# Packing a spectrum of 192 channels into 128 partitions with column tiles

## The chip, the cores and the metric

The kernel runs on one core of one Trainium2 chip, as one program. The metric is the device time in microseconds (us), the median of three runs. A run with the hardware profiler gives the profile and the trace from which all views below are taken. TensorE is called PE in them, its weight loads PEld, VectorE DVE, ScalarE ACT, GpSimd POOL and the queue that issues the transfers SP.

## The reference

Thirty-two images of 56x56 positions with 96 channels pass through two layers. The first is a layer norm, a 3x3 convolution and a SiLU with a residual. The second treats the 3136 positions of an image as a sequence, and has a spectral attention and a quantized feed-forward network. The part that the change touches is in the spectral attention:

```
h = relu(bn1(x @ w1.T))                      # 96 -> 192 channels
X = fft(h, axis=positions)                   # a transform per channel
xr = relu(X.real * rd - X.imag * idg + rb)   # rd, idg, rb, ib: one number per channel
xi = relu(X.imag * rd + X.real * idg + ib)
y = ifft(xr + 1j * xi).real
o = y @ w2.T                                 # 192 -> 96 channels, then bn2
```

All of this is float32. Since y is real, the transform back keeps one half of a Hermitian spectrum; the kernel folds that into two terms for the real and imaginary part of each stored frequency.

## The kernel before

**The transform in two factors.** 3136 is split into 112 x 28. `transform_a` multiplies by w1 and does the first factor (112 points) and writes the result to a buffer `da` in memory; read back transposed, it is ready for the second factor (28 points). The 56 first-factor frequencies are handled in 28 pairs, `PG = 4` pairs are one unit, and an image has `NS = 7` units, so the kernel has 32 x 7 = 224 units.

**One unit of `spectrum`.** `back` brings the unit's rows, `ats[g]`, with 112 partitions by 4 pairs by 192 channels. `forward(g, i)` runs for i = 0 and i = 1, the two halves of 96 channels: four matmuls (line 379), one per pair, each with 96 channels as the stationary operand and a table of 112 columns (`fb_sb`, 114 in the first unit of an image) as the moving one. The result `px` has the 96 channels on the partitions and 4 pairs x 2 (real, imaginary) x 56 frequencies along the free dimension. Then come three ACT instructions (lines 389 to 391, into `av`), three DVE instructions (lines 393 to 395, into `sv`), one more ACT instruction (line 396) and two DVE instructions (lines 397 and 398) that write `gt`, all on 96 partitions by 224 elements, with the channel's numbers as per-partition scalars out of `par_sb` and `scal`.

`inverse(g)` runs a step later. For each of the four pairs it multiplies `gt` (96 channels by 112 frequencies, the stationary operand) with w2 (96 columns, the moving operand), for i = 0 and i = 1 into the same accumulator `pg`: eight matmuls (line 406). ACT copies the accumulator to `gw` (line 408), four matmuls with `ib_sb` do the second factor back (line 411, `pe`), ACT copies that to `es` (line 413), and a transfer brings it to the buffer `de`.

**Records of one matmul.** A float32 matmul of this program stands in the trace as two weight loads and two MATMUL records; 224 units x 8 matmuls of `px` are 3584 records. A transpose has one record. A record is called a pass below.

**What else runs.** A loop over the images is a pipeline by hand: while an image's spectrum runs, `filler` emits parts of the convolution of a later image (`conv_part`: lines 328 to 337) and of its input (`take_in`, `make_image`: lines 257 to 299). After the spectrum stage the loop emits, group by group, `forth` (the next image's `transform_a`), `back` (the transform out, line 431) and `ffn` (lines 437 to 460). A scheduler then orders the instructions of each engine by its own estimates, so the order on an engine is not the order of the source. `px` shares the accumulators of tag "c" (two buffers) with `ph` and `py`; `pg` and `pe` share tag "b" (two buffers) with `pa` and `po`.

Of the kernel before, what the change touches and what calls it, by code (L numbers as in the profile page):

```python
# [38 lines left out]
F32 = mybir.dt.float32  # L39
# [3 lines left out]
ALU = mybir.AluOpType  # L43
AX = mybir.AxisListType

C = 96
# [5 lines left out]
PG = 4  # L52
NS = NP // PG
H = 192
# [8 lines left out]
LN_CHUNKS = ((0, 8), (8, 16), (16, 24), (24, 28))  # L63


LN_W, LN_B, CONV_B, B_IN, BN1, BN2, RD, RB, NPAR = 0, 1, 2, 3, 5, 13, 17, 21, 25


def width(p):

    return 2 * N2 + (p < PG)


def first(p):

    return 2 * (2 * N2 * p + min(p, PG))


@with_exitstack
def hybrid_kernel(ctx: ExitStack, tc: tile.TileContext, x, par, w_in, conv_w, w1, w2, fw1, fb1, fw2, fb2, fa, fb, ib, ia, on, out):  # L80
    nc = tc.nc
    nb = x.shape[0]

    const = ctx.enter_context(tc.tile_pool(name="const", bufs=1))


    ident = const.tile([128, 128], F32, name="ident")
# [8 lines left out]
    fb_sb = const.tile([112, first(NP)], F32, name="fb_sb")  # L96
    ib_sb = const.tile([114, NP, 112], F32, name="ib_sb")

    par_sb = const.tile([C, NPAR], F32, name="par_sb")
    nc.sync.dma_start(par_sb, par)  # L100
    convb = par_sb[:, CONV_B : CONV_B + 1]

    wp = const.tile([128, 7, C], F32, name="wp")
    w1a = const.tile([C + 1, H], F32, name="w1a")
    w2a = const.tile([C, 2, C], F32, name="w2a")
    w1q = const.tile([C, FF], F8, name="w1q")
    w2q = const.tile([128, 3, C], F8, name="w2q")
    b1q = const.tile([128, 3], F32, name="b1q")
# [2 lines left out]

    stages = [const.tile([C, 2, G4, P58], F32, name=f"stage{i}") for i in range(2)]
    ys = [const.tile([113, G4, C], F32, name=f"y{i}") for i in range(4)]
    scal = const.tile([C, 3, 2], F32, name="scal")

    dconst = ctx.enter_context(tc.tile_pool(name="dconst", bufs=1, space=bass.MemoryType.DRAM))
    imgs = [dconst.tile([C, (P58 + 1) * P58], F32, name=f"img{i}") for i in range(3)]
# [1 line left out]
    with tc.tile_pool(name="setup", bufs=1) as sp, tc.tile_pool(  # L119
        name="setup_ps", bufs=2, space=bass.MemoryType.PSUM  # L120
# [13 lines left out]
        for g in range(2):  # L134
            ps = spp.tile([128, 512], F32, tag="ps", name=f"ps_wt{g}")
# [6 lines left out]
        for k in range(9):  # L142
            ps = spp.tile([128, 512], F32, tag="ps", name=f"ps_we{k}")
# [12 lines left out]
        def bn_fold(scale, bias, at, n):  # L156

            p = par_sb[:, at : at + 4 * n]
            nc.vector.tensor_scalar(scale, p[:, 3 * n : 4 * n], EPS, None, ALU.add)
            nc.gpsimd.tensor_tensor(scale, scale, mhalf[:C, :n], ALU.pow)  # L160
            nc.vector.tensor_tensor(scale, scale, p[:, 0:n], ALU.mult)
            nc.vector.tensor_tensor(bias, p[:, 2 * n : 3 * n], scale, ALU.mult)
            nc.vector.tensor_tensor(bias, p[:, n : 2 * n], bias, ALU.subtract)
# [7 lines left out]
        for g in range(2):  # L171
            nc.vector.tensor_scalar(w1s[:, g, :C], w1s[:, g, :C], s1[:, g : g + 1], None, ALU.mult)
            nc.vector.tensor_copy(w1s[:, g, C : C + 1], o1[:, g : g + 1])
            ps = spp.tile([128, 512], F32, tag="ps", name=f"ps_w1{g}")
            nc.tensor.transpose(ps[: C + 1, :C], w1s[:, g, :], ident[:C, :C])
            nc.vector.tensor_copy(w1a[:, g * C : (g + 1) * C], ps[: C + 1, :C])
        ps = spp.tile([128, 512], F32, tag="ps", name="ps_w1c")
# [4 lines left out]
        s2 = sp.tile([C, 1], F32, name="s2")  # L182
        o2 = sp.tile([C, 1], F32, name="o2")
        bn_fold(s2, o2, BN2, 1)
        w2s = sp.tile([C, H], F32, name="w2s")
        nc.sync.dma_start(w2s, w2)
        nc.vector.tensor_scalar(w2s, w2s, s2, None, ALU.mult)
        for g in range(2):
            ps = spp.tile([128, 512], F32, tag="ps", name=f"ps_w2{g}")
            nc.tensor.transpose(ps[:C, :C], w2s[:, g * C : (g + 1) * C], ident[:C, :C])  # L190
            nc.vector.tensor_copy(w2a[:, g, :], ps[:C, :C])
        ps = spp.tile([128, 512], F32, tag="ps", name="ps_o2")
        nc.tensor.transpose(ps[:1, :C], o2, ident[:C, :C])
        row = sp.tile([1, G4, C], F32, name="row")
# [3 lines left out]
            nc.sync.dma_start(y[112:113], row)  # L198


        nc.vector.tensor_scalar(scal[:, 0, :], par_sb[:, RD : RD + 2], 2.0, None, ALU.mult)
        nc.vector.tensor_scalar(scal[:, 1, :], par_sb[:, RB : RB + 2], 2.0, None, ALU.mult)
        nc.vector.tensor_scalar(scal[:, 2, :], par_sb[:, RD : RD + 2], -1.0, None, ALU.mult)


        f1 = sp.tile([128, 3, C], F32, name="f1")
# [3 lines left out]
        for k in range(3):  # L210
            ps = spp.tile([128, 512], F32, tag="ps", name=f"ps_f1{k}")
            nc.tensor.transpose(ps[:C, :128], f1[:, k, :], ident)
            nc.vector.tensor_copy(w1q[:, k * 128 : (k + 1) * 128], ps[:C, :128], saturate=False)
            ps = spp.tile([128, 512], F32, tag="ps", name=f"ps_f2{k}")
# [28 lines left out]
    work = ctx.enter_context(tc.tile_pool(name="work", bufs=2))  # L243
    w3 = ctx.enter_context(tc.tile_pool(name="w3", bufs=3))
    sums = ctx.enter_context(tc.tile_pool(name="sums", bufs=8))
    psum = ctx.enter_context(tc.tile_pool(name="psum", bufs=1, space=bass.MemoryType.PSUM))
    psum2 = ctx.enter_context(tc.tile_pool(name="psum2", bufs=2, space=bass.MemoryType.PSUM))
# [112 lines left out]
    def spectrum(da, de, b):  # L360


        rows = da.rearrange("n (k p) c -> (n k) p c", p=NP)
        gt, ats = {}, {}

        def back(g):
            ats[g] = w3.tile([112, PG, H], F32, tag="at", name=f"at_{b}_{g}")
            nc.sync.dma_start(ats[g], rows[:, g * PG : (g + 1) * PG, :])

        for g in range(3):  # L370
            back(g)
        yield

        def forward(g, i):
            w = width(g * PG)
            px = psum2.tile([C, PG, 2, w], F32, tag="c", name=f"px_{b}_{g}_{i}")
            for j in range(PG):
                p = g * PG + j
                nc.tensor.matmul(  # L379
                    px[:, j], ats[g][:, j, i * C : (i + 1) * C], fb_sb[:, first(p) : first(p + 1)], start=True, stop=True  # L380
                )
            if i == 0:
                gt[g] = w3.tile([C, 2, PG, 2, w], F32, tag="gt", name=f"gt_{b}_{g}")
            rd, idg = par_sb[:, RD + i : RD + i + 1], par_sb[:, RD + 2 + i : RD + 3 + i]
            rb, ibi = par_sb[:, RB + i : RB + i + 1], par_sb[:, RB + 2 + i : RB + 3 + i]
            rd2, rb2, mrd = (scal[:, k, i : i + 1] for k in range(3))
            re, im = px[:, :, 0, :], px[:, :, 1, :]
            av = work.tile([C, 3, PG, w], F32, tag="av", name=f"av_{b}_{g}_{i}")
            nc.scalar.activation(av[:, 0], im, AF.Abs, scale=idg)
            nc.scalar.activation(av[:, 1], re, AF.Relu, scale=rd2, bias=rb2)  # L390
            nc.scalar.activation(av[:, 2], re, AF.Identity, scale=idg, bias=ibi)  # L391
            sv = work.tile([C, 3, PG, w], F32, tag="sv", name=f"sv_{b}_{g}_{i}")
            nc.vector.scalar_tensor_tensor(sv[:, 0], re, rd, av[:, 0], ALU.mult, ALU.add)  # L393
            nc.vector.scalar_tensor_tensor(sv[:, 1], im, mrd, av[:, 2], ALU.mult, ALU.add)
            nc.vector.scalar_tensor_tensor(sv[:, 2], im, rd, av[:, 2], ALU.mult, ALU.add)  # L395
            nc.scalar.activation(sv[:, 1], sv[:, 1], AF.Relu)
            nc.vector.scalar_tensor_tensor(gt[g][:, i, :, 0, :], sv[:, 0], rb, av[:, 1], ALU.add, ALU.max)
            nc.vector.scalar_tensor_tensor(gt[g][:, i, :, 1, :], sv[:, 2], 0.0, sv[:, 1], ALU.max, ALU.subtract)  # L398

        def inverse(g):  # L400
            k = 2 * width(g * PG)
            pg = psum2.tile([k, PG, C], F32, tag="b", name=f"pg_{b}_{g}")
            for j in range(PG):
                for i in range(2):
                    lhs = gt[g][:, i, j].rearrange("c r k -> c (r k)")
                    nc.tensor.matmul(pg[:, j, :], lhs, w2a[:, i, :], start=(i == 0), stop=(i == 1))  # L406
            gw = work.tile([k, PG, C], F32, tag="gw", name=f"gw_{b}_{g}")
            nc.scalar.copy(gw, pg)
            pe = psum2.tile([112, PG, C], F32, tag="b", name=f"pe_{b}_{g}")
            for j in range(PG):  # L410
                nc.tensor.matmul(pe[:, j, :], ib_sb[:k, g * PG + j, :], gw[:, j, :], start=True, stop=True)  # L411
            es = work.tile([112, PG, C], F32, tag="es", name=f"es_{b}_{g}")
            nc.scalar.copy(es, pe)
            nc.sync.dma_start(de[g * PG : (g + 1) * PG].rearrange("p m c -> m p c"), es)
            del gt[g]

        for g in range(NS + 1):
            if g < NS:
                forward(g, 0)
                forward(g, 1)  # L420
            if g + 3 < NS:
                back(g + 3)
            yield
            if g >= 1:
                inverse(g - 1)
            yield
# [297 lines left out]
```

## Time and profile before

| what | value |
|---|---|
| device time, median of 3 | 4036.05 us (4034.21 to 4038.8) |
| span of the profiled execution | 4024.5 us, granted TensorE clock 0.982 |
| PE busy | 3664.8 us, 91% |
| PE weight loads busy | 2484.2 us, 62% |
| DVE busy | 2667.9 us, 66% |
| ACT busy | 2193.7 us, 55% |
| POOL busy | 1285.9 us, 32% |
| mean rate of the transfers | 137 GB/s |

A share of busy time is a mean over stages with different limits. The first `px` record starts at 203.0 us and the last at 3957.8 us, and between them the stages of the images repeat about every 120 us. The end of a PE record is modelled and records overlap, so a row's count times its mean is more than its busy time; the distance from one start to the next is what a pass takes of the engine.

### The profile page before, as it was taken

Reading aid. Unit: us, or ns where it says so; the run is one execution under the profiler, and the core shown is the slowest. Engines: PE = TensorE matmul, PEld = TensorE weight load, DVE = VectorE, ACT = ScalarE, POOL = GpSimd, SP = SyncE. Lnnn points to the kernel's source line nnn. Section 1 sums busy time; section 2 is a strip of 40 time slices with the busy share of each in tenths; the row PEclk is TensorE's granted clock in tenths of the full one; section 3 lists DMA queues with packets and bytes.
Section 4 is the critical chain, followed back from the end, with each engine's and each line's share of the span. In section 5 each row is a group of like instructions: output and inputs, shape, how many; then the busy total and the mean of one; then the engine's idle time right before and its main releaser. Section 6 shows DMA issues by size and latency. Waiting matters only on the chain. (4 is left out here: it accounts for less than half of the span.)

```text
span 4024.5 us, 70610 instructions
## 1 busy us (share of the span) xinstructions
PE 3664.8 (91%) x22229; PEld 2484.2 (62%) x22229; DVE 2667.9 (66%) x9014; ACT 2193.7 (55%) x5154; POOL 1285.9 (32%) x1004
## 2 busy tenths in 40 slices
PE   3899999999999999999999999999999999999987
PEld 2466665666665666665666655666655666665665
DVE  2256776766776766776766776766776766776666
ACT  0355555565555555555555555655555555555564
POOL 1222333332333332333322333322333332333222
PEclk9999999999999999999999999999999999999996
DMA  5454455555555555555545455545455555455531
GB/s 152 128 143 135 129 148 143 146 139 137 136 140 143 149 138 137 136 139 141 145 136 138 129 145 144 148 136 138 130 149 144 147 139 136 134 142 144 143 88 52
DMA packets 582156, 550.04 MB, mean 137 GB/s; under 512 B 171960, under 2 KB 534680, under 8 KB 581272
## 3 DMA queue, kind: packets, MB, share of 16 engines
q1 hardware_dynamic: 579906, 543.45, 49.5%
q8 instruction: 180, 2.95, 0.3%
q10 hardware_dynamic: 1880, 2.09, 0.2%
q14 instruction: 190, 1.56, 0.1%
HBM read 346.93 MB, written 197.99 MB: 135 GB/s over the span
## 5 line engine op out<-in xcount | busy, mean ns | idle before, releaser
L328 PE MATMUL cv<-k,wp 128*96 128x448 f32 (+1 forms) x3136 | 1370.5, 551 | 19.3 <-ACT s L330 12.6
L328 PEld LDWEIGHTS cv<-k,wp 128*96 128x96 f32 (+1 forms) x3136 | 463.2, 165 | 382.6 <-issue 326.3
L443 ACT CAST h<-pf 128x448 f16<-128x448 f32 x672 | 358.5, 533 | 434.3 <-PE pf L441 413.9
L432 DVE TENSOR_TENSOR t<-py,t 112x384 f32<-112x384 f32 x224 | 124.2, 555 | 628.3 <-PE py L431 628.3
L280 POOL TENSOR_TENSOR xn_c<-t,mu_c 112x768 f32<-112x768 f32 (+1 forms) x128 | 169.1, 1321 | 1027.2 <-DVE var_a L263 826.3
L379 PE MATMUL px<-fb_sb,at 112*96 112x112 f32 (+1 forms) x3584 | 429.6, 262 | 24.9 <-DVE sv L395 19.1
L379 PEld LDWEIGHTS px<-fb_sb,at 112*96 112x96 f32 x3584 | 382.4, 164 | 78.6 <-issue 31.6
L406 PE MATMUL pg<-w2a,gt 96*112 96x96 f32 (+1 forms) x3584 | 416.0, 264 | 13.0 <-DVE gt L398 10.8
L354 ACT ACTIVATE h<-ph,rs_b 112x192 f32<-112x192 f32 x896 | 325.0, 419 | 187.0 <-PE ph L351 175.9
L453 PEld LDWEIGHTS <-hq 128*112 128x112 fp8e5 x2688 | 209.0, 135 | 330.8 <-DVE hq L446 281.2
L351 PE MATMUL ph<-w1a,n2t 97*112 97x192 f32 x1792 | 366.0, 333 | 42.3 <-DVE t L432 41.6
L406 PEld LDWEIGHTS pg<-w2a,gt 96*112 96x112 f32 (+1 forms) x3584 | 382.3, 179 | 27.4 <-PE st L336 12.9
L269 POOL TENSOR_TENSOR rs_a<-var_a,mhalf 112x8 f32<-112x8 f32 (+1 forms) x128 | 199.4, 1558 | 610.9 <-DVE var_a L268 566.2
L445 DVE TENSOR_SCALAR h<-h,b1q 128x448 f16<-128x448 f16 x672 | 350.9, 522 | 62.7 <-ACT h L443 59.3
L330 ACT ACTIVATE s<-cv,par_sb 96x448 f32<-96x448 f32 x224 | 141.4, 631 | 457.3 <-PE cv L328 457.3
L453 PE MATMUL po<-w2q,hq 128*112 128x96 fp8e5 x2688 | 252.2, 221 | 141.3 <-DVE hq L446 133.2
L269 POOL TENSOR_TENSOR rs_b<-var_b,mhalf 112x8 f32<-112x8 f32 (+1 forms) x128 | 192.5, 1504 | 580.7 <-DVE var_b L268 414.5
L356 PE MATMUL pa<-h,fa_sb 112*112 112x384 f32 x896 | 369.4, 508 | 6.3 <-ACT h L354 1.2
L460 POOL TENSOR_TENSOR o<-t,y 112x384 f32<-112x384 f32 x224 | 201.1, 898 | 449.5 <-DVE y L459 259.7
L351 PEld LDWEIGHTS ph<-w1a,n2t 97*112 97x112 f32 x1792 | 281.7, 177 | 93.7 <-DVE t L432 61.1
L446 DVE CAST hq<-h 128x448 fp8e5<-128x448 f16 x672 | 314.8, 469 | 16.1
L393 DVE SCALAR_TENSOR_TENSOR sv<-px,par_sb,av 96x224 f32<-96x224 f32 (+1 forms) x448 | 197.9, 442 | 174.7 <-ACT av L391 173.8
(106 smaller groups left out, 6389.7 us busy)
## 6 DMA issues: line engine op xcount, KB each, us to landing
k<-img SPq DMA_DIRECT2D x2464, 58.0 KB
da<-u SPq DMA_DIRECT2D x224, 336.0 KB
at<-da SPq DMA_DIRECT2D x224, 336.0 KB
img<-stage SPq DMA_DIRECT2D x224, 174.0 KB
de<-es SPq DMA_DIRECT2D x224, 168.0 KB
y<-de SPq DMA_DIRECT2D x224, 168.0 KB
out<-o SPq DMA_DIRECT2D x224, 168.0 KB
xl<-in_x SPq DMA_DIRECT2D x96, 336.0 KB
```

Of the source, the lines that this page charges most:

```text
L269: nc.gpsimd.tensor_tensor(rs, var, mhalf[:, :n], ALU.pow)
L328: nc.tensor.matmul(ps, wp[: seen.shape[0], k, :], seen, start=(k == 0), stop=(k == 6))
L351: nc.tensor.matmul(ph[:, j, :], n2t[:, 2 * j2 + j, :], w1a, start=True, stop=True)
L354: nc.scalar.activation(h[:, j], ph[:, j], AF.Relu, scale=rs[:, 2 * j2 + j : 2 * j2 + j + 1])
L356: nc.tensor.matmul(pa, fa_sb, h, start=True, stop=True)
L379: nc.tensor.matmul(px[:, j], ats[g][:, j, i * C : (i + 1) * C], fb_sb[:, first(p) : first(p + 1)], start=True, stop=True)
L406: nc.tensor.matmul(pg[:, j, :], lhs, w2a[:, i, :], start=(i == 0), stop=(i == 1))
L443: nc.scalar.copy(h1, pf)
L445: nc.vector.tensor_scalar(h2, h1, b1q[:, k : k + 1], 0.0, ALU.add, ALU.max)
L446: nc.vector.tensor_copy(hq[:, k, :], h2, saturate=False)
L453: nc.tensor.matmul(po[:, j, :], hq[:, k, j * N1 : (j + 1) * N1], w2q[:, k, :], start=(k == 0), stop=(k == 2))
L460: nc.gpsimd.tensor_tensor(o, tg, y2, ALU.add)
```

## The change

It cuts the 192 channels of a unit otherwise: not 96 + 96, but 128 + 64. In `forward(g, 0)` 128 channels of four pairs lie on 128 partitions. In `forward(g, 1)` the other 64 channels lie twice on the partitions: pairs 0 and 1 on partitions 0 to 63, pairs 2 and 3 on partitions 64 to 127, so the tile has two pairs along the free dimension where it had four. Its four matmuls have 64 stationary columns each; the ones for the upper half write partitions 64 to 127 of the accumulator, through the upper column tile of PE's array. The purpose is to use all partitions in the elementwise work on the spectrum.

In `inverse` the 64-channel part of two pairs (one on each half of the partitions) is one stationary operand, and w2 for these channels is laid out as a block-diagonal moving operand `w2y` of 2 x 96 columns, so one matmul does both pairs. Two matmuls then add the 128 channels of each of the two pairs with `w2x`. The scalars per channel come in a tensor of their own, `spar`, laid out for the 128 partitions.

```diff
         def forward(g, i):
             w = width(g * PG)
-            px = psum2.tile([C, PG, 2, w], F32, tag="c", name=f"px_{b}_{g}_{i}")
-            for j in range(PG):
-                p = g * PG + j
-                nc.tensor.matmul(
-                    px[:, j], ats[g][:, j, i * C : (i + 1) * C], fb_sb[:, first(p) : first(p + 1)], start=True, stop=True
-                )
-            if i == 0:
-                gt[g] = w3.tile([C, 2, PG, 2, w], F32, tag="gt", name=f"gt_{b}_{g}")
+            n = PG >> i
+            px = psum2.tile([128, n, 2, w], F32, tag="c", name=f"px_{b}_{g}_{i}")
+            for j in range(n):
+                for half in range(i + 1):
+                    p = j + 2 * half
+                    rows = slice(64 * half, 64 * half + 64) if i else slice(0, 128)
+                    nc.tensor.matmul(
+                        px[rows, j],
+                        ats[g][:, p, 128 * i : 128 + 64 * i],
+                        fb_sb[:, first(g * PG + p) : first(g * PG + p + 1)],
+                        start=True,
+                        stop=True,
+                    )
+            gt[g, i] = w3.tile([128, n, 2, w], F32, tag=f"gt{i}", name=f"gt_{b}_{g}_{i}")
...
-            av = work.tile([C, 3, PG, w], F32, tag="av", name=f"av_{b}_{g}_{i}")
+            av = work.tile([128, 3, n, w], F32, tag="av", name=f"av_{b}_{g}_{i}")
...
-            sv = work.tile([C, 3, PG, w], F32, tag="sv", name=f"sv_{b}_{g}_{i}")
+            sv = work.tile([128, 3, n, w], F32, tag="sv", name=f"sv_{b}_{g}_{i}")
...
         def inverse(g):
             k = 2 * width(g * PG)
-            pg = psum2.tile([k, PG, C], F32, tag="b", name=f"pg_{b}_{g}")
-            for j in range(PG):
-                for i in range(2):
-                    lhs = gt[g][:, i, j].rearrange("c r k -> c (r k)")
-                    nc.tensor.matmul(pg[:, j, :], lhs, w2a[:, i, :], start=(i == 0), stop=(i == 1))
+            pg = psum2.tile([k, 2, 2, C], F32, tag="b", name=f"pg_{b}_{g}")
+            for j in range(2):
+                lhs = gt[g, 1][:, j].rearrange("c r k -> c (r k)")
+                nc.tensor.matmul(pg[:, :, j, :], lhs, w2y, start=True, stop=False, skip_group_check=True)
+                for half in range(2):
+                    lhs = gt[g, 0][:, 2 * half + j].rearrange("c r k -> c (r k)")
+                    nc.tensor.matmul(pg[:, half, j, :], lhs, w2x, start=False, stop=True, skip_group_check=True)
```

In the setup, `w2x` and `w2y` are made from w2 (one memset, one copy and two more copies on DVE), and one more transfer loads `spar`.

## The prediction

> **What bounds the kernel now.** I read the page first: busy time, then its costliest groups.
>
> ```profile
> PE 3664.8 (91%) x22229; PEld 2484.2 (62%) x22229; DVE 2667.9 (66%) x9014; ACT 2193.7 (55%) x5154; POOL 1285.9 (32%) x1004
> ...
> L379 PE MATMUL px<-fb_sb,at 112*96 112x112 f32 (+1 forms) x3584 | 429.6, 262 | 24.9 <-DVE sv L395 19.1
> ...
> L406 PE MATMUL pg<-w2a,gt 96*112 96x96 f32 (+1 forms) x3584 | 416.0, 264 | 13.0 <-DVE gt L398 10.8
> ```
>
> PE is the busiest engine, and the idle time in front of the two matmul groups that change is only 24.9 + 13.0 us in all. Next I asked for busy time in two stretches of one mid-run image: its spectrum stage (first `px` to last `pg`) and the rest. Columns: stretch, length, PE, PEld, DVE, ACT, POOL busy, clock, DMA share, GB/s.
>
> ```profile
> 2027.40:2066.80 39.40, 38.43 (x337) 34.27 (x336) 30.71 (x103) 32.61 (x82) 4.71 (x4) 1.00 0.43 113
> 2066.80:2148.10 81.30, 73.38 (x360) 41.90 (x359) 53.43 (x177) 35.80 (x80) 35.12 (x27) 1.00 0.56 153
> ```
>
> In the spectrum stage PE is busy 38.43 of 39.40 us, while DVE has 8.7 us and ACT 6.8 us to spare. So here time on PE is paid, and time on DVE or ACT is paid only through waits. Last, the PE timeline of that stage (start, length, records merged):
>
> ```profile
> 2054.61 0.93 PE L379 MATMUL px<-fb_sb,at 112*96 112x112 f32 x8
> 2055.37 1.72 PE L406 MATMUL pg<-w2a,gt 96*112 96x96 f32 x16
> ...
> 2084.87 1.46 PE L351 MATMUL ph<-w1a,n2t 97*112 97x192 f32 x8
> ```
>
> A stretch of n passes lasts n - 1 start-to-start distances and one record. So a `px` pass takes (0.93 - 0.26) / 7 = 0.096 us, a `pg` pass (1.72 - 0.26) / 15 = 0.097 us, a pass of 192 moving columns (1.46 - 0.33) / 7 = 0.161 us. `px` moves 112 columns over 96 stationary ones, `pg` 96 over 112, and both take the same: a pass costs its longer side, as the load of the next weights runs beside the stream of this one. `pg`'s load side gives 0.097 / 112 = 0.87 ns a column. The stage's records at such distances (112 `px`, 112 `pg`, 48 `pe`, 15 `cv` at 0.375, 32 transposes `tp`, 10 `st` at 0.08, 8 `ph`) add up to 37.1 us; the other 2.3 us, 74 us over 32 images, are short stalls behind DVE and ACT.
>
> [...]
>
> **The change part by part.** All counts are per unit, and there are 224.
>
> *`px`, 128 channels.* Four matmuls, 8 passes, now bound by the load of 128 columns: 128 x 0.87 = 0.111 us. 8 x (0.111 - 0.096) = +0.12 us.
>
> *`pg`.* 16 passes of 0.097 us become 4 of 192 columns at 0.161 and 8 at 0.097: 0.644 + 0.776 - 1.552 = -0.13 us. Two matmuls fewer, but the moving columns stay 768. With `px` the sum is -0.01 us, -2 us in all: as good as nothing.
>
> *`px`, 64 channels, on alternating column tiles.* Still 8 passes of 112 moving columns. One after the other they cost what they did, 0.77 us. If a pass runs beside its neighbour on the other tile, the order lower, lower, upper, upper, lower, ... leaves 5 of 8 distances: 0.48 us, -0.29 us. Bounds: 0 and -65 us in all. I take half, -32 us: passes of one tile still wait for each other, and a load may wait for the pass ahead of it.
>
> *Mode switches.* In the instruction order of the built program the four matmuls of 64 columns nearly always stand together, with full-width work before and after: 452 switches. The kernel before has no row for a switch. Lower bound 0. Upper bound: the rest of the running record (0.259 - 0.096 = 0.163 us, until its modelled end), then a load that no stream hides (64 columns 0.056, 128 columns 0.111, mean 0.084 us), together 0.247 us, 112 us in all. I take 0.1 us, +45 us: the modelled end of a record is later than the array needs, and part of the load can overlap. What stands behind a switch is the whole PE queue, so this is paid in full.
>
> *Elementwise work of the second half.* 224 elements become 112 in five DVE and four ACT instructions. [...] On ACT, copies of 384 and 448 elements (lines 357 and 342, 481 and 536 ns) give 0.86 ns an element, 96 ns each, 0.39 us a unit. Over 7 units DVE falls from 30.7 to about 26.6 us and ACT from 32.6 to 29.9 us of a stage. That is 216 us of work, none of it on PE; it pays only where PE waited for `sv`, `gt` or `gw`. Bounds: 0, and the 74 us of stalls. The page's idle time in front of `px`, `pg` and `pe` (24.9 + 13.0 + 1.7 us) is 40 us of it; I take 40 us.
>
> *The rest.* The first factor, feed-forward, convolution and transfers are untouched; in the built order a spectrum stage keeps its 7 convolution matmuls, 32 transposes and 4 `ph` matmuls. The `gt` tiles take less memory. Setup has four small DVE instructions and one transfer more: +1 us.
>
> Sum: -2 - 32 + 45 - 40 + 1 = -28 us, 4036 to **4008 us**.
>
> **The rivals.**
>
> *The tiles overlap and the switch is cheap.* For it: [...] a load already overlaps a stream in every pass seen here. Against it: alternating float32 passes have never been seen here[...]. -2 - 65 + 452 x 0.05 (+23) - 40 + 1 = -83 us: 3953 us.
>
> *The switch takes the place of the waits: slower.* Passes of 64 columns run one after the other, and every change of mode costs 0.2 us. For it: PE has no slack in this stage, and a record in flight lasts 0.16 us past the next start. Against it: it needs both bad answers. -2 + 0 + 90 - 30 + 1 = +59 us: 4095 us. With the full 0.247 us and no relief it would be 4147 us.
>
> *Nothing to measure.* Overlap at half, and a switch of 0.16 us (+72 us), cancel the relief: -1 us, 4035 us. What speaks for it is that the width terms cancel by themselves.
>
> **How the numbers follow.** Forecast 0.37, fast rival 0.2, slower rival 0.33, no change 0.1. The forecast's own width (overlap and switch each out by half) puts a fifth of it across the line, but the slower rival has a mild part too, with overlap helping; so faster by over 0.2% 0.52, within it 0.1, slower 0.38. The range runs from just under the fast rival to a little over the slower one, 3945 to 4105 us; what is left out is full overlap with a free switch, and the full switch cost without relief.
>
> **What would show it.** The `px` passes of 128 columns should start 0.11 us apart, the 192-column `pg` passes 0.16 us. In the 64-column group, upper and lower passes that start within a few tens of ns of each other show overlap; 0.096 us apart shows none. The distance across a change of mode, less the pass's own, is the switch: above 0.15 us the forecast is lost. DVE should fall by about 130 us in all and ACT by about 87 us. The spectrum stage should be some 0.9 us shorter, the rest of an image unchanged; if the rest moves by more than a microsecond an image, the scheduler's new order did it and the step "the rest" is wrong.

## The result: slower by 1.3%, and all of the loss outside the stage that changed

| | before | after |
|---|---|---|
| device time, median | 4036.39 us (4034.21 to 4038.8) | 4087.19 us (4086.63 to 4087.61) |
| ratio to before | | 1.0126, interval 1.0110 to 1.0142 |
| span of the profiled execution | 4024.5 us | 4085.7 us |
| mean granted TensorE clock | 0.982 | 0.967 |
| PE busy | 3664.8 us | 3707.8 us |
| DVE, ACT busy | 2667.9, 2193.7 us | 2583.1, 2132.0 us |

The page of the changed kernel: busy time, the granted clock in 40 slices, and the two groups that the text below comes back to. The changed kernel's line numbers are 11 to 22 higher around here: `ph` is line 362 (351 before), `t` 454 (432), `d_a` 278 (267), `var_a` 279 (268), the GpSimd multiplication `xn_c` 292 (281).

```profile
PE 3707.8 (91%) x21333; PEld 2421.2 (59%) x21333; DVE 2583.1 (63%) x9017; ACT 2132.0 (52%) x5154; POOL 1288.6 (32%) x1004
...
PEclk9999999999999999999999999999999999999997
...
L362 PE MATMUL ph<-w1a,n2t 97*112 97x192 f32 x1792 | 366.5, 336 | 74.4 <-DVE t L454 74.4
L395 PE MATMUL px<-fb_sb,at 112*64 112x112 f32 (+3 forms) x3584 | 392.4, 278 | 26.5 <-issue 15.9
```

DVE and ACT have less to do, PE has 896 records fewer, and yet PE is busy longer. That is what a lower clock looks like: the same passes last longer. (The first experiment below shows it: with the same PE instructions in the same order and fewer stretches at half clock, PE is busy for 3646.8 us.) In slices of a tenth the clock hides it; the mean clock of the span, 0.967, does not. The idle time ahead of `ph`, a group that the change does not touch, is the other sign.

The same two stretches of one mid-run image as in the prediction, now of the changed kernel (length, then PE, PEld, DVE, ACT, POOL busy, clock, DMA share, GB/s):

```profile
2060.90:2100.30 39.40, 37.93 (x310) 31.38 (x308) 27.39 (x103) 30.62 (x82) 4.59 (x4) 1.00 0.40 104
2100.30:2184.00 83.70, 76.83 (x360) 43.36 (x359) 52.96 (x177) 35.87 (x80) 35.51 (x27) 0.96 0.56 153
```

The spectrum stage is as long as it was; the rest of the image has grown from 81.30 to 83.70 us, with the same 360 PE records in it, and its clock is 0.96 where it was 1.00.

Over 26 images from the middle of the run I measured from first `px` to last `pg` (stage), from there to the next stage (rest), the stall of PE ahead of the second pair of `ph` matmuls (the distance between the two starts, less the 0.161 us that a pass takes), and the stretches in which the trace gives the clock as 0.5. Every one of these stretches in the middle of the run lasts 3.413 us; they are called half-clock windows here.

| per image, us | stage | rest | sum | stall ahead of `ph` | half-clock windows in 26 images |
|---|---|---|---|---|---|
| before | 39.22 | 81.42 | 120.64 | 1.58 | 9 |
| after | 39.13 | 83.79 | 122.92 | 2.73 | 48 |

Of the 2.28 us that an image gained, the stall is 1.15 us and the stage -0.09 us. What is left, 1.22 us, goes with 39 more windows; that is 0.8 us for each, found by difference and not measured by itself. A pass inside a window takes about twice as long from start to start (`ph` 0.320 us for 0.163, `px` of the kernel before 0.188 for 0.096), so my estimate of what one can cost is at most half its length, 1.71 us, and less where PE would have waited anyway.

**What stands ahead of `ph`.** Part of the waits of the kernel before (total us, times, longest):

```profile
PE ph L351 <- DVE t L432: 41.6, 29, 2.6
```

And of the changed kernel:

```profile
PE ph L362 <- DVE t L454: 74.4, 29, 2.6
PE tp_im L300 <- POOL xn_a L292: 31.0, 2, 29.0
PE pe L433 <- ACT gw L430: 25.8, 40, 0.7
```

Both have 29 such waits, the longest 2.6 us in both; the changed kernel has the long form of it every time. `t` (adding `py` out of an accumulator) frees the accumulator of tag "c" that the next `ph` needs, and it stands in DVE's queue behind the small statistics of the next input. The timeline of DVE and POOL at that place in one image, kernel before (start, length):

```profile
888.00 0.72 DVE L257 BATCH_NORM_STATS2 st_a<-xl 112x6 f32<-112x96 f32 x4
...
889.11 0.24 DVE L257 BATCH_NORM_STATS2 st_a<-xl 112x6 f32<-112x96 f32 x1
...
889.59 0.17 DVE L267 SCALAR_TENSOR_TENSOR d_a<-d_a 112x8 f32<-112x8 f32 x1
889.79 0.17 DVE L268 SCALAR_TENSOR_TENSOR var_a<-var_a,d_a 112x8 f32<-112x8 f32 x1
889.87 1.47 POOL L281 TENSOR_TENSOR xn_c<-xn_c,rs_c 112x768 f32<-112x768 f32 x1
889.88 0.55 DVE L432 TENSOR_TENSOR t<-py,t 112x384 f32<-112x384 f32 x1
```

The same place and image in the changed kernel:

```profile
901.00 1.36 DVE L268 BATCH_NORM_STATS2 st_a<-xl 112x6 f32<-112x96 f32 x8
...
902.86 1.47 POOL L292 TENSOR_TENSOR xn_c<-xn_c,rs_c 112x768 f32<-112x768 f32 x1
902.93 1.42 DVE L278 SCALAR_TENSOR_TENSOR d_a<-d_a 112x8 f32<-112x8 f32 x1
904.28 0.55 DVE L454 TENSOR_TENSOR t<-py,t 112x384 f32<-112x384 f32 x1
904.88 0.90 PE L362 MATMUL ph<-w1a,n2t 97*112 97x192 f32 x4 [2.57 <-DVE t L454]
```

An operation on 112 x 8 elements takes 0.17 us when it starts ahead of GpSimd's multiplication and 1.42 us when it starts 0.07 us behind it; it then ends with it. `t` and `ph` wait behind. At this place it is `d_a` or `var_a` that stretches, in every image that has the long stall; both operands of either are in SBUF. In the whole of both traces `t` out of `py`, with one operand in an accumulator, never lasts over 0.56 us, though 74 (before) and 29 (after) of them start while GpSimd writes a tile `xn`, 0.1 us or more ahead of its end; and the `bn_stats` of `t`, with one SBUF input, take 0.24 us in the median then as at other times. A rule by operands does not follow: `h` of the feed-forward (line 445), with one SBUF tensor and a column of scalars, takes 1.14 us in the median when it starts there in the kernel before, ends 0.13 us after the write, and takes 0.33 us with none beside it. What makes an operation wait is not shown.

Why it starts behind is in the order of DVE's instructions. From the end of `var_c`, which lets GpSimd go on to `rs_c` (1.64 us) and `xn_c`, DVE runs part of the eight `bn_stats` of the next input group, one `t`, and then the statistics. In the kernel before, 5 of the eight stand there in 20 of the 26 images, and nothing is stretched; 6 in the other six images, and `var_a` is. In the changed kernel the scheduler has put all 8 there, in every image, and `d_a` is stretched in every image: 3 more starts 0.16 us apart are 0.48 us, more than the 0.28 us by which this operation was ahead. Why the scheduler put them there is not shown.

**What the stall does to the clock.** Three consecutive windows of 3.41 us in the changed kernel around the same place (length, PE, PEld, DVE, ACT, POOL busy, clock, DMA share, GB/s):

```profile
902.65:906.06 3.41, 1.18 (x8) 1.09 (x9) 3.41 (x12) 0.67 (x3) 2.16 (x3) 1.00 0.79 210
906.06:909.47 3.41, 3.41 (x10) 1.87 (x9) 1.39 (x7) 2.33 (x6) 2.70 (x2) 0.50 0.50 129
909.47:912.88 3.41, 3.41 (x23) 1.99 (x22) 3.39 (x14) 0.91 (x2) 0.70 (x1) 1.00 0.74 151
```

PE is busy for 1.18 of 3.41 us in the first; in the second its clock is 0.50 and it gets 10 records done, where the third, back at full clock, has 23 (the records are not all of one kind).

**Inside the stage.** PE's timeline of one unit and a later step of the changed kernel (start, length, records merged):

```profile
858.66 1.07 PE L395 MATMUL px<-fb_sb,at 112*128 112x112 f32 x8
859.57 0.35 PE L300 MATMUL tp_im<-ident,xn_a 112*96 112x112 f32 x2
859.85 0.60 PE L395 MATMUL px<-fb_sb,at 112*64 112x112 f32 x8
860.39 0.40 PE L300 MATMUL tp_im<-ident,xn_a 112*96 112x112 f32 x2
860.62 0.49 PE L424 MATMUL pg<-w2y,gt 128*112 128x192 f32 x2
...
867.83 1.03 PE L433 MATMUL pe<-gw,ib_sb 112*112 112x96 f32 x8 [0.69 <-ACT gw L430]
```

With the working of the prediction, the eight 128-channel passes are (1.07 - 0.28) / 7 = 0.113 us apart. The eight 64-channel passes take 0.60 us with the last one's end, where eight of 96 channels took 0.93. The single starts show why: inside a unit they are, in the median, 7, 140, 7, 89, 7, 89 and 7 ns apart. No other two PE records of the trace start less than 40 ns apart, so I read each pair as passes of opposite column tiles, which start as good as together; the records do not name the tile. The last line is a new wait, taken up below.

### The profile page after: what moved, and what is told of

The parts are those of the page before. It is cut to its first block, busy times and chain, and to the rows that moved or that the text cites. A ratio compares the mean times of both kernels' runs of the same rounds, so it can differ in the third digit from the quotient of the medians.

```text
span 4085.7 us, 69055 instructions
## 1 busy us (share of the span) xinstructions
PE 3707.8 (91%) x21333; PEld 2421.2 (59%) x21333; DVE 2583.1 (63%) x9017; ACT 2132.0 (52%) x5154; POOL 1288.6 (32%) x1004
## 4 chain that ended last, share of the span: by engine, by line
PE 57%; DVE 25%; ACT 6%; POOL 4%; issue 2%; DMA 0%; SPq 0%; POOLq 0%; ACTq 0%; DVEq 0%
PE cv L339 19%; PE px L395 7%; PE pa L367 6%; DVE h L467 5%; PE ph L362 5%; PE pe L433 5%; DVE hq L468 4%; POOL rs_b L280 4%; PE py L453 3%; PE pg L427 3%; PE pg L424 3%; PE po L475 3%; PE tp_n L300 2%; DVE var_c L279 2%; DVE n3t L459 2%
## 5 line engine op out<-in xcount | busy, mean ns | idle before, releaser
L339 PE MATMUL cv<-k,wp 128*96 128x448 f32 (+1 forms) x3136 | 1397.7, 559 | 19.9 <-ACT s L341 12.6
L395 PE MATMUL px<-fb_sb,at 112*64 112x112 f32 (+3 forms) x3584 | 392.4, 278 | 26.5 <-issue 15.9
L367 PE MATMUL pa<-h,fa_sb 112*112 112x384 f32 x896 | 387.3, 529 | 5.8 <-ACT h L365 1.2
L395 PEld LDWEIGHTS px<-fb_sb,at 112*64 112x64 f32 (+1 forms) x3584 | 316.9, 165 | 104.0 <-issue 47.1
L467 DVE TENSOR_SCALAR h<-h,b1q 128x448 f16<-128x448 f16 x672 | 340.3, 506 | 44.1 <-ACT h L465 42.5
L411 DVE SCALAR_TENSOR_TENSOR sv<-px,spar_sb,av 128x224 f32<-128x224 f32 (+1 forms) x448 | 174.1, 389 | 245.8 <-ACT av L409 245.7
L468 DVE CAST hq<-h 128x448 fp8e5<-128x448 f16 x672 | 305.2, 454 | 17.1
L368 ACT COPY u<-pa 112x384 f32<-112x384 f32 x448 | 215.6, 482 | 161.1 <-PE pa L367 152.9
L463 PE MATMUL pf<-n3t,w1q 96*128 96x448 fp8e5 x672 | 250.6, 373 | 17.0 <-DVE n3t L459 14.4
```

Source lines behind the costliest of these rows:

```text
L339: nc.tensor.matmul(ps, wp[: seen.shape[0], k, :], seen, start=(k == 0), stop=(k == 6))
L367: nc.tensor.matmul(pa, fa_sb, h, start=True, stop=True)
L368: nc.scalar.copy(u[:, 2 * j2 : 2 * j2 + 2, :], pa)
L395: nc.tensor.matmul(px[rows, j], ats[g][:, p, 128 * i : 128 + 64 * i], fb_sb[:, first(g * PG + p) : first(g * PG + p + 1)], start=True, sto ...
L463: nc.tensor.matmul(pf, w1q[:, k * 128 : (k + 1) * 128], n3t, start=True, stop=True)
L467: nc.vector.tensor_scalar(h2, h1, b1q[:, k : k + 1], 0.0, ALU.add, ALU.max)
```

## The experiments

First the two that decide, then what led to them, then the tests of the clock and of the stage. The kernel before was timed again beside every series, and ratios are to that time: 4031.46 us for the next two experiments, 4032.42 us for the kernel before with both edits and for the new wait inside the stage, 4033.97 us for all others.

**Let GpSimd start later, in the changed kernel.** Only GpSimd's queue gets two instructions more, on `rs_c` (`mu_rs[1]`); the order on all other engines stays as it was.

```diff
         if mu:
             nc.gpsimd.tensor_tensor(xc, t[:, :, :C], mu, ALU.subtract)
-        nc.gpsimd.tensor_tensor(xc, xc if mu else t, rs, ALU.mult)
+        [nc.gpsimd.tensor_scalar(mu_rs[1], mu_rs[1], 1.0, None, ALU.mult) for _ in range(2 if kind == "c" and i == 1 else 0)]; nc.gpsimd.tensor_tensor(xc, xc if mu else t, rs, ALU.mult)
```

> The changed kernel with work added and nothing else: two multiplications by 1.0 of 8 elements on GpSimd (some 0.2 us each) ahead of the xn_c multiplication of an image's second group. The order of the instructions on TensorE, VectorE, ScalarE and the transfer queue is the same. In the changed kernel d_a (line 278) of that place starts 0.06 to 0.07 us after xn_c in all 27 images and takes 1.42 us. Theory (d_a waits for xn_c[...], and the ph matmuls wait behind it): with xn_c some 0.45 us later d_a starts first and takes 0.17 us, the stall of TensorE ahead of ph goes from 2.7 to about 1.3 us in every image, the page's wait of ph for DVE t from 74 to 35 to 45 us, half-clock windows at that place vanish, and the time is that of the kernel with the statistics on GpSimd, 3990 to 4015 us. Rival (the statistics on GpSimd helped by relieving DVE of six instructions, or by another order): more GpSimd work can't help, 4080 to 4100 us.

Measured: 4014.52 us (4010.37 to 4015.82), ratio to before 0.9953 (0.9939 to 0.9968). Adding work on GpSimd took 73 us off the changed kernel. Its waits, and the same place in the same image:

```profile
PE ph L362 <- DVE t L454: 37.8, 29, 1.3
```

```profile
887.21 0.55 POOL L292 TENSOR_SCALAR rs_c<-rs_c 112x8 f32<-112x8 f32 x2
887.27 0.17 DVE L278 SCALAR_TENSOR_TENSOR d_a<-d_a 112x8 f32<-112x8 f32 x1
887.35 0.55 DVE L454 TENSOR_TENSOR t<-py,t 112x384 f32<-112x384 f32 x1
887.85 1.48 POOL L292 TENSOR_TENSOR xn_c<-xn_c,rs_c 112x768 f32<-112x768 f32 x1
```

`d_a` is back at 0.17 us in all images, `t` follows 0.08 us later. The stall ahead of `ph` is 1.47 us, the rest of an image 81.15 us, below the kernel before's 81.42, and 6 windows are left of 48, none of them behind `ph`. PE is busy for 3646.8 us, 61 us less than in the changed kernel, with the same instructions in the same order. The rival is out: GpSimd has more to do, and the order on PE, DVE and ACT is unchanged.

**Put the collision into the kernel before.** Three of the eight `bn_stats` of that group are computed twice. ACT and GpSimd keep their order, PE too but for two records of the setup.

```diff
-        for j in range(n):
+        for j in [*range(n), *range(3 if kind == "a" and i == 1 else 0)]:
             nc.vector.bn_stats(st[:, j].rearrange("p h s -> p (h s)"), t[:, j, :C])
```

> The kernel before, with three of the eight bn_stats of the input group concerned computed a second time on DVE (0.16 us from start to start, 96 instructions in all). The order on TensorE, GpSimd and ScalarE is the same but for the setup; on DVE 8 or 9 of these instructions now stand between var_c and d_a, where 5 or 6 stood, and 8 stand in the changed kernel. Theory: d_a now starts after xn_c in all images, its 1.4 us stand ahead of t, the stall ahead of ph is about 2.7 us in every image (5 to 6 in 26 images had that before), +1.1 us an image, and half-clock windows come with it (9 before; 15 to 40 now): 4036 + 32 x 1.1 + (6 to 31) x 1.7 = 4080 to 4125 us; without any spectrum packing it has the changed kernel's loss. Rival (the loss of the changed kernel comes from its TensorE work or the mode switches, not from this place): 96 x 0.16 us of DVE work with DVE at 66%, 4035 to 4045 us.

Measured: 4087.91 us (4087.43 to 4089.67), ratio 1.0139 (1.0122 to 1.0156). That is the changed kernel's time, 4087.19 us, without a single instruction of the change. Its waits and the place in one image:

```profile
PE ph L351 <- DVE t L432: 75.0, 29, 2.6
```

```profile
893.89 0.17 DVE L262 TENSOR_TENSOR d_a<-st_a 112x8 f32<-112x8 f32 x1
893.90 1.50 POOL L281 TENSOR_TENSOR xn_c<-xn_c,rs_c 112x768 f32<-112x768 f32 x1
893.98 1.45 DVE L263 SCALAR_TENSOR_TENSOR var_a<-st_a 112x8 f32<-112x8 f32 x1
895.35 0.15 DVE L267 SCALAR_TENSOR_TENSOR d_a<-d_a 112x8 f32<-112x8 f32 x1
895.43 0.54 DVE L432 TENSOR_TENSOR t<-py,t 112x384 f32<-112x384 f32 x1
```

Here it is `var_a` of line 263 that starts behind `xn_c` and ends with it (in six of the 26 images, `d_a` of line 262). The stall is 2.80 us in the mean, long in every image (1.58 before), the rest of an image 83.75 us (changed kernel: 83.79), and there are 34 windows for 9. That the two times agree to a microsecond is chance, since the changed kernel has 48. So 15 us of DVE work, on an engine that is busy for two thirds of the time, cost 56 us.

**The input statistics on GpSimd, in both kernels.** This came first, after the trace had shown the stretched operation. The four small operations of these statistics leave DVE, and six take their place on GpSimd.

```diff
+        if kind == "a":
+            nc.gpsimd.tensor_tensor(d, st[:, :, 0, 1], st[:, :, 1, 1], ALU.subtract)
+            ...
+            nc.gpsimd.tensor_tensor(rs, var, mhalf[:, :n], ALU.pow)
+            return None, rs
```

> The changed kernel, with the small operations of the input statistics (kind a) on GpSimd instead of DVE, so that no two-operand DVE instruction of that kind waits behind a GpSimd one. Theory 1 (stall and clock): the changed kernel's loss is one longer stall per image in front of a ph matmul (2.7 us where the kernel before mostly has 1.3 us) and the half-clock windows of 3.41 us that follow such stalls (46 in mid-run against 12). Here that stall should fall to about 1.3 us and the windows behind it should go: 4087 - 1.35 x 29 - 23 x 1.3 = about 4020 us, under 20 half-clock windows in mid-run. Theory 2 (tiles): the loss is on PE itself, from changes of tile mode and the wider loads; then the time stays within 10 us of 4087.

Measured: 3994.06 us (3992.72 to 3999.22), ratio 0.9907 (0.9892 to 0.9922). The stall is 1.40 us, 2 windows are left, and an image takes 119.73 us. This fits the collision, but it changed the work and the order of DVE too; the kernel with GpSimd delayed is the cleaner proof.

> The same edit in the kernel before. Theory 1: its stall is already 1.3 us in most images, only six images with 2.6 us gain, and the windows stay near 10: 4020 to 4036 us, so the two kernels come within 10 us of each other. Theory 2: the difference of 51 us between the two kernels stays.

Measured: 4049.62 us (4045.52 to 4051.27), ratio 1.0041 (1.0026 to 1.0056). As a control it failed. The stall ahead of `ph` did fall, to 0.88 us, but the scheduler ordered the spectrum stage differently: PE now waits 2.27 us an image between transposes and `px` (0.97 before), and the stage has 40.26 us instead of 39.22. An edit of a few tiny instructions elsewhere moved the stage by a microsecond: here too an order changed that the edit was not meant to touch.

**Convolution matmuls ahead of the last feed-forward groups, in both kernels.** A second long stall, 2.15 us ahead of `po` some 117 us into an image, precedes the windows found there. With this edit five `cv` matmuls stand ahead of it where two stood:

```diff
+            if g == NG + LAG:
+                filler(g + 1)
```

> The changed kernel, with the last part of the convolution filler of an image emitted ahead of the last feed-forward group, so that five cv matmuls stand in front of po instead of two, and fill the 2.15 us stall ahead of a spectrum stage. Nothing else moves. Theory 1: that stall goes (-2.15 x 29 = -62 us) and so do the half-clock windows behind it (about 23 x 1.3 = -30 us): about 3995 us, and the windows left are those behind the other stall. If only the stall counts and the clock costs nothing: 4025 us. Theory 2 says nothing against the stall, but expects no change in the clock: 4025 us.

Measured: 3966.21 us (3965.17 to 3967.56), ratio 0.9836 (0.9821 to 0.9851). All 21 windows that are left follow the stall ahead of `ph`, which is still 2.72 us.

> The same edit in the kernel before. Theory 1: -62 us for the stall and about 6 windows fewer, -8 us: about 3966 us. Theory 2: -62 us, 3974 us, still 51 us below the changed kernel with the same edit.

Measured: 3945.93 us (3944.22 to 3950.86), ratio 0.9787 (0.9771 to 0.9803), 7 windows, all behind `ph` in the six images where this kernel has the collision. With the same edit the changed kernel stays 20 us behind: the edit takes away the other stall in both, and the collision remains in one in every image. Both times are below the lowest of their forecasts, by 29 us in the changed kernel and by 20 us in the kernel before; where the rest comes from stays open.

**Both edits together.**

> The changed kernel with both edits: the small operations of the input statistics on GpSimd, and the last part of the convolution filler ahead of the last feed-forward group. Theory 1: the run with the first edit has 119.7 us an image, of which the 2.15 us stall ahead of the spectrum stage now goes too, and no stall over 2 us is left, so no half-clock windows in mid-run: 3994 - 2.15 x 29 = about 3930 us. If the two edits do not add up (a new stall in their place): 3950 us or more.

Measured: 3923.43 us (3917.39 to 3924.72), ratio 0.9724 (0.9709 to 0.9738). No window is left in the 26 images. This is the fastest version, and it beats both kernels.

> The kernel before with both edits of the fastest changed kernel (input statistics on GpSimd, five convolution matmuls ahead of the last feed-forward groups). Two readings of what the packing is worth by itself. If it is worth what its matmuls and its elementwise work save in the spectrum stage and nothing else, about 1 us an image once neither kernel has a long stall, then this kernel is some 25 to 45 us slower than the changed one with the same edits (3923.43): 3950 to 3970 us. If the packing is worth nothing and only the order of the small statistics counts, the two are the same within 0.3%: 3912 to 3935 us. The statistics on GpSimd moved the order of the spectrum stage in the kernel before (1 us an image longer there), so a part of a difference may come from that; the trace's spectrum stage against 39.2 us tells it.

Measured: 3960.78 us (3958.16 to 3962.71), ratio 0.9827 (0.9812 to 0.9841). It is 37 us behind the changed kernel with the same two edits. But its stage is 40.68 us for 38.83, and 1.6 us of the difference are waits between transposes and `px`. With the statistics on GpSimd these rose in this kernel (from 0.97 to 2.27 us), and not in the changed one. So this pair does not tell what the packing is worth; the best version without it is the one with the convolution edit only, at 3945.93 us.

**More PE time in the stage, in both kernels.** The stationary operand of `pe` is padded from 112 to 128 columns, which should lengthen PE's work by about 0.8 us an image and keeps the order on every engine.

```diff
-            pe = psum2.tile([112, PG, C], F32, tag="b", name=f"pe_{b}_{g}")
+            pe = psum2.tile([128, PG, C], F32, tag="b", name=f"pe_{b}_{g}")
...
-            nc.scalar.copy(es, pe)
+            nc.scalar.copy(es, pe[:112])
```

> The kernel before, with the stationary operand of every pe matmul padded from 112 to 128 columns; the instruction order stays the same. This adds 56 passes x 0.014 us = 0.78 us of PE work to an image, 25 us in all. Theory 1 (the windows in which the clock may fall lie on a fixed grid of 3.413 us, and which of them fall on a stall depends on the period of an image against this grid): a replay of the trace's PE gaps against such a grid, at half clock after each window with less than 0.42 of activity, gives 6 half-clock windows in 26 images as it is and 17 with the addition, 1.5 us more an image, so +44 us: about 4078 us. Plain theory (what is added is paid once): +23 to +25 us, 4058 us. If the stage is bound by waits and not by PE: 0.

Measured: 4052.28 us (4049.73 to 4053.01), ratio 1.0045 (1.0028 to 1.0061), 18 us above the kernel before. The count of windows came out (16), the time did not.

> The same padding in the changed kernel, +0.78 us of PE work an image. Theory 1: an image now takes 122.9 us, 36 windows of 3.413 us; the replay gives fewer half-clock windows with the addition and the same time, so 0 to +12 us: 4087 to 4099 us, with fewer than 45 half-clock windows in 26 images. Plain theory: +23 to +25 us, 4111 us, and as many windows as before.

Measured: 4139.76 us (4133.04 to 4143.5), ratio 1.0261 (1.0246 to 1.0276), 65 windows. Both forecasts failed: I had thought that other places of the stalls in the grid of windows would leave fewer of them. The replay's limit of 0.42 of activity was an estimate; in the traces of the two kernels PE is busy for 0.24 to 0.49 of the window ahead of each half-clock window in mid-run. How many windows a kernel gets depends on where its stalls meet the grid, and I could not work that out ahead of a run. The changed kernel is an unlucky case: its image of 122.92 us is 36.01 windows long, so that the stall meets the grid at nearly the same place in every image, and 26 of its 48 windows follow the stall ahead of `ph`, one in each of the 26 images. The other 22 follow the stall ahead of `po`, which is as long as in the kernel before (2.15 us), where 5 do. So the change in the length of an image also moved a stall that the edit had left alone to places of the grid where half clock follows. Whether the windows themselves hold the image at this length was not tried. In the padded changed kernel all 26 stalls of either place are followed by half clock, and 13 of these stretches last two windows: in them the stall still reaches 0.03 to 0.14 of a window into the first.

**Stalls of chosen length.** A kernel of its own, which leaves out the whole computation: bursts of float32 matmuls, and between them two ACT instructions on which the next burst waits.

> Not this computation at all, only PE and ACT: 216 bursts of 20 float32 matmuls of 448 columns (15 us), and between bursts PE waits for two ACT instructions, the second over 560 to 2900 elements, so that PE stands still for about 1.1 to 3.2 us, 24 times for each of nine lengths. Theory 1: stalls under 2.0 us are never followed by a half-clock window; from about 2.0 us on, 0.4 of them are, rising to 0.8 at 3.2 us, each half-clock window is 3.413 us long and starts on one fixed grid. Rival: only a whole idle window of 3.41 us or more lowers the clock, so none of these stalls does.

Measured, 24 stalls of each length (23 of the longest): none of the 72 stalls from 1.2 to 1.9 us was followed by a half-clock window; of 2.0 us 2, of 2.2 us 3, of 2.4 us 7, of 2.6 us 9, of 2.9 us 14 and of 3.2 us 17 were. All half-clock stretches begin on one grid of 3.413 us, within 0.0005 of a window, and each lasts one window, but for one of 123 us at the end, where PE has nothing left to do. What decides here is the share of a window that one stall covers: the smallest with a half-clock window after it is 0.53, the largest without is 0.55. So between such bursts a stall needs some 1.8 us in one window of the grid. The rival is out: 52 stalls, all shorter than a window, were followed by half clock. In the kernel before, no short stall ahead of `ph` (1.3 us) was followed by half clock in the 26 images, and 4 of the 6 long ones (2.6 us) were.

In the kernels themselves this share decides only roughly. In the kernels before and after the change, stalls that cover 0.51 of a window were followed by half clock, and others of up to 0.60 were not. In the kernel before with both edits no stall at `ph` or `po` has half clock behind it, but 7 waits between four transposes and `px` do: six of 1.57 us, 0.46 of a window, and one of 1.82 us; others of the same length there do not. What else counts is not shown.

**The new wait inside the stage.** In the sixth unit `pe` waits for the copy `gw`, which stands on ACT behind the next unit's `av` operations. The copy goes to DVE there, on top of the statistics on GpSimd:

```diff
-            nc.scalar.copy(gw, pg)
+            (nc.vector.tensor_copy if g == NS - 2 else nc.scalar.copy)(gw, pg)
```

> The changed kernel with the input statistics on GpSimd, and in the sixth unit of each image the copy of pg to gw on DVE in place of ACT. Theory: the saving of the matmuls in the spectrum stage was given back as a wait of pe for that copy, 0.87 us an image, since ACT has the next unit's av operations ahead of it. Then the wait falls to about 0.3 us, the stage is 0.4 to 0.8 us an image shorter, and the time is 13 to 26 us below that of the kernel without this edit (3994.06): 3968 to 3981 us. Rival: the wait only moves to another instruction (sv or gt queue behind the copy on DVE), the stage stays within 0.2 us and the time within 8 us: 3986 to 4002 us.

Measured: 4069.04 us (4065.37 to 4075.38), ratio 1.0099 (1.0082 to 1.0116), 75 us above the same kernel without the edit. Some of its waits:

```profile
PE ph L371 <- ACT h L374: 27.6, 31, 1.2
PE ph L371 <- DVE sv L422: 21.0, 31, 0.7
...
PE pe L442 <- ACT gw L439: 4.3, 9, 0.7
```

The wait of `pe` fell from 25.6 to 4.3 us, as meant. But the scheduler, which now saw `gw` later, put four `ph` matmuls ahead of `pe`, and these wait 48.6 us in places where none waited. The stage went from 38.77 to 40.57 us, and the windows from 2 to 19. Neither forecast was right: the wait was real, and its removal brought an order with two others.

## Why the prediction was wrong, step by step

**128 channels of `px`, and `pg`.** Right for `px`: the passes start 0.112 us apart in the median (0.111). `pg` was a little too cheap: a pass of 192 columns takes 0.162 us ahead of one of 96 (0.161), but 0.167 to 0.180 us ahead of the other one of 192, and 0.25 us where it comes straight after the 64-column passes. That is 0.36 us an image, some 11 us in all.

**64 channels on alternating tiles.** Mis-sized, on the good side. That tiles overlap at all was an estimate, as no loop instruction of the kernel before has 64 columns or fewer. I took half of the gain that full overlap would give, 0.14 us a unit; the passes start in pairs 7 ns apart, and first to last start is 0.346 us where 7 x 0.096 = 0.672 stood: 0.33 us a unit.

**Mode switches.** Right: 0.1 us predicted, an estimate as well. The start after a switch comes 0.189 us after the last 64-column one, where most transitions between full-width passes have 0.096 to 0.098, and the first 64-column pass comes 0.205 us after a 128-channel one, where 0.112 is the rule: 0.09 us each way. So a change of mode costs about one pass; what happens in that time is not shown. Switches included, the 64-channel part takes 0.63 us of PE where it took 0.77, -31 us in all; the steps had given -32 + 45 = +13.

**Elementwise relief.** The work fell nearly as said. The five DVE groups went from 964 to 841 us, -124 us for a predicted 130; one operation at 112 elements is 0.118 us shorter than at 224 (line 412, 0.443 and 0.325). The saving on DVE was an estimate; the trace of the kernel before has these five at 224 and 228 elements only. ACT fell by 62 us for 87: the three operations that read `px` became 0.07 to 0.08 us shorter, where 0.096 was foreseen, and the one that reads `sv` 0.10 us. So an element out of the accumulator costs 0.64 to 0.74 ns in this range, less than the 0.86 ns that I took from longer copies. The step failed where it turned work into time. I expected 40 us of waits to go; stalls over 0.2 us in a stage went from 1.42 to 2.20 us an image, +25 us. The stalls ahead of `px` and `pg` fell only from 1.42 to 1.33 us, as I read it since a pass that comes sooner found its producer not ready, and that of `pe` behind `gw` is new, 0.87 us. So the stage is 0.09 us shorter, not 0.9: with -2 us for the full-width passes as predicted, -31 for the 64-column part, +11 for `pg` and +25 for the waits the sum is about zero, and 3 us were measured. The 40 us of relief are thus a step that failed by itself. That PE's saving was given back to waits is read from the trace; the one attempt to take it out of that wait moved the order and settled nothing more.

**"The rest untouched" is the step that failed the forecast.** The instructions of the rest are the same (the setup has three more on DVE, 9017 for 9014, where four were counted), but their order on DVE is not: 8 `bn_stats` instead of 5 between `var_c` and `d_a`. The rest took 2.37 us more in each of the 26 images, 62 us, against a whole forecast of -28. The prediction had named this as its test, "if the rest moves by more than a microsecond an image, the scheduler's new order did it", and I had compared the order of PE only. The delay of GpSimd (-73 us) and the repeated `bn_stats` (+56 us in the kernel before) show it to be the cause of the whole loss: with the collision gone the changed kernel is 0.5% faster than before (0.9953), some 17 us. That is not the gain that was foreseen. An image in mid-run is 0.36 us shorter than in the kernel before, and 0.27 us of this lies in the rest, where the kernel before still has its own collision in 6 of 26 images. The stage gives 0.08 us, some 3 us in all; the remainder of the 17 us comes from the first and last images. So with the rest untouched the forecast of -28 us would still have failed, at the step above.

**The rivals.** The slower one, at 4095 us, came close in time for a reason that was wrong: tiles do overlap and the switch costs 0.09 us, not 0.2. The fast rival had the tiles right (-65 us for a measured -73) and the switch at half its price (452 x 0.05 for 0.09); what it shared with the forecast, the relief and the untouched rest, was wrong. What would have warned ahead of the result was in the kernel before's own trace: 29 waits of `ph` with a total of 41.6 us and a longest of 2.6 us, so mostly short and a few twice as long. Here the wait with two sizes at one place in the code sat on an edge: 5 or 6 `bn_stats`.

## What to carry to other kernels

Where a scheduler orders the instructions, a change that saves work in one stage can also reorder engines that it does not touch; compare the order of every engine, not only that of the busiest, and search for waits whose longest is far above their mean: such a place may be close to an edge, as it was here. Where something that TensorE needs is queued behind a small VectorE operation, see in the trace on which side of a long GpSimd instruction that operation starts: here one on 112 x 8 elements with both operands in SBUF that starts 0.04 us ahead of the GpSimd multiplication of 1.47 us keeps its 0.16 us, and one that starts 0.06 us behind takes 1.43 us. And a stall of TensorE of 2 us or more can be paid twice, once as a stall and once as a window at half clock; whether it is depends on how much of one window it fills: some 0.53 between bursts of matmuls, 0.46 to 0.60 in the kernels.

## What the runs showed of the hardware that I had not expected

- 8 elements per partition took 1.42 us on DVE instead of 0.17 us, when they started 0.07 us after a GpSimd multiplication of 1.47 us.
- Between bursts of matmuls one stall that covers 0.53 to 0.55 of a 3.413 us window is enough to halve the clock of the next window; in the kernels the limit lay between 0.46 and 0.60. With PE busy for the whole of that window the clock came back at once; where the stall still covered 0.03 or more of it, the padded kernel stayed at half clock for one window more.
- Float32 passes of 64 columns start in pairs 7 ns apart, which I read as one on each column tile; entering or leaving that mode costs 0.09 us each way.
